# Down projection of whole batches by seven products of half width, in a linear attention and dense expert kernel

## The chip, the cores and the metric

The kernel runs on one core of a Trainium2 chip. The metric is device time in microseconds (us) of one execution; the time of a kernel is the median of its runs. One execution was also taken by the hardware profiler, and its trace gives the start and duration of every instruction on each engine: TensorE (PE, with its weight loads as PEld), VectorE (DVE), ScalarE (ACT), GpSimd (POOL) and SyncE (SP, which here only issues DMAs).

## The reference

Eight batches of 512 tokens of 128 channels go through a linear attention and then through eight dense experts; both are normalized and added to their input. Everything is fp32.

```python
def block(x):                                  # x: (8, 512, 128)
    x = x + layernorm(attn(layernorm(x)))
    return x + layernorm(ffn(layernorm(x)))

def attn(x):                                   # 4 heads of 32
    xn = layernorm(x) * gamma + beta
    q, k, v = split(xn @ w_qkv)
    k = softmax(k, over tokens)
    context = k^T v  (per head)
    return (q * 32**-0.5) @ context @ w_out + b_out + x

def ffn(x):                                    # 8 experts, 512 wide
    return sum(silu(x @ Wg[e]) * (x @ Wu[e]) @ Wd[e] for e in range(8))
```

## The kernel before

All expert weights stay in SBUF. The experts' work is cut into units: batches 0 and 7 are two units of 256 tokens each, batches 1 to 6 one unit of 512, ten units in all. A unit has 32 steps, one for each expert and each 128 of its 512 inner channels. A step (lines 621 to 639) makes g and u in PSUM on TensorE (lines 627 and 629, weights 128x128, the unit's tokens as columns), silu(g) on ScalarE (631), h = silu(g) * u on VectorE (633), and the down projection on TensorE (`down`, line 582), which adds wd^T h into one PSUM bank (acc) over all 32 steps. `down` is issued two steps late (LAG), so that h is ready. g and u have two PSUM banks each, acc one, everything else three (pool ps).

There is no scheduler: the order on each engine is the order in which the program issues, written by hand. `between(n)` is a set of generators; each step of the loop advances each of them by one `yield`, and so lays a piece of other work behind that step's h. While unit n runs its steps, `attention(b + 1)` prepares the next batch and `finish` ends the last one. `attention` normalizes x (statistics and application on VectorE, the reciprocal root as a power on GpSimd, lines 182 to 200), brings the tokens to channels, makes keys and their exponential (397 to 402), then g_ps, c_ps, m_ps, wa_ps (428 to 449), which fold context and output weights into one 128x128 matrix, and y (476); then follow two more normalizations with the residual on GpSimd (490) between them. `finish` normalizes the sum of the experts, adds the residual on GpSimd (529) and stores it.

Transpositions of batches 2 to 7 are made by VectorE in blocks of 32x32, and the blocks are brought to their places by `carry` (line 211): a store of the tile to DRAM and four loads from it, issued by SP. Generators wait LANDING steps for them. Batches 0 and 1 are transposed by TensorE. Batch 0's attention is a function of its own (`opening`) with nothing beside it. `finish_last` ends the last unit.

Of the kernel before, what the change touches and what calls it, by code (L numbers as in the profile page):

```python
# [1 line left out]

# [13 lines left out]
def kernel(  # L16
# [32 lines left out]

    nc = tc.nc  # L50
# [5 lines left out]
    Q = 32  # L56
    NQ = P // Q
    LANDING = 4
    BY_TENSORE = (0, 1)
# [8 lines left out]
    work = ctx.enter_context(tc.tile_pool(name="work", bufs=2))  # L68
    small = ctx.enter_context(tc.tile_pool(name="small", bufs=3))
    hp = ctx.enter_context(tc.tile_pool(name="hp", bufs=4))  # L70
    dram = ctx.enter_context(tc.tile_pool(name="dram", bufs=4, space=bass.MemoryType.DRAM))
# [3 lines left out]
    ps = ctx.enter_context(tc.tile_pool(name="ps", bufs=3, space=bass.MemoryType.PSUM))  # L75
# [74 lines left out]
    def keep_warm(moving, count=1):  # L150

        t = ps_acc.tile([P, N], F32, tag="acc", name="unread")
        for i in range(count):
            nc.tensor.matmul(
                t[:, : moving.shape[1]], moving[:, :P], moving,
                start=(i == 0), stop=(i == count - 1),
            )


    def norm_stats(src, name):  # L160

        n = src.shape[1]
        stats = small.tile([P, n, 6], F32, tag=f"stats{n}", name=f"stats_{name}")
        mv = small.tile([P, n, 2], F32, tag=f"mv{n}", name=f"mv_{name}")
        for j in range(n):
            nc.vector.bn_stats(stats[:, j, :], src[:, j])
# [8 lines left out]
    def pair_stats(src, name):  # L175
# [19 lines left out]
        return mv, rstd[:, :n], rstd[:, n:]  # L195

# [51 lines left out]
    def opening():  # L248
# [12 lines left out]
        v = const.tile([P, N], F32, name="v_0")  # L261
        qT = const.tile([P, N], F32, name="qT_0")
        x1 = work.tile([P, NJ, C], F32, tag="x1", name="x1_0")
        x1b = work.tile([P, NJ, C], F32, tag="x1b", name="x1b_0")
# [3 lines left out]
        yn = work.tile([P, NJ, C], F32, tag="yn", name="yn_0")  # L268
        z = work.tile([P, NJ, C], F32, tag="z", name="z_0")
        zT = work.tile([P, NQ, NJ, Q], F32, tag="zT", name="zT_0")  # L270
# [103 lines left out]
    def attention(b):  # L374
        xt = xs[b]
# [7 lines left out]
        if b in BY_TENSORE:  # L383
            xh_ps = transpose4(flat(xh), f"xh_ps_{b}")
            nc.scalar.activation(xnT, xh_ps, AF.Identity, bias=beta_sb, scale=gamma_sb)
        else:
            xhT = work.tile([P, NQ, P], F32, tag="xhT", name=f"xhT_{b}")
            to_channels(xh, xhT, f"xh_blk_{b}")
            for _ in range(LANDING):
                yield  # L390
            nc.scalar.activation(
                by_block(xnT), xhT.rearrange("c a (j i) -> c a j i", j=NJ),
                AF.Identity, bias=beta_sb, scale=gamma_sb,
            )
# [13 lines left out]
        x1b = work.tile([P, NJ, C], F32, tag="x1b", name=f"x1b_{b}")  # L408
# [4 lines left out]
        if b in BY_TENSORE:  # L413
            ek_ps = transpose4(ekT, f"ek_ps_{b}")
            nc.vector.tensor_copy(
                ek.rearrange("p b (j k) -> p j b k", j=NJ),
                ek_ps.rearrange("p (j b k) -> p j b k", j=NJ, b=NQ),
            )
            yield
            yield  # L420
        else:
            to_tokens(by_block(ekT), ek, f"ek_blk_{b}")
            for _ in range(LANDING):
                yield
# [26 lines left out]
        nc.vector.tensor_copy(wa, wa_ps[:, :C])  # L451
        yield
        x2 = xp.tile([P, NJ, C], F32, tag="x2", name=f"x2_{b}")
        x2s[b] = x2
        y = work.tile([P, NJ, C], F32, tag="y", name=f"y_{b}")
        yn = work.tile([P, NJ, C], F32, tag="yn", name=f"yn_{b}")
        z = work.tile([P, NJ, C], F32, tag="z", name=f"z_{b}")
        zT = work.tile([P, NQ, NJ, Q], F32, tag="zT", name=f"zT_{b}")
        lags = [after_wa(b, lo, hi, xt, xnT, wa, x1b, x2, y, yn, z, zT) for lo, hi in WHOLE]
        while lags:  # L460
            if next(lags[0], "end") == "end":
                lags.pop(0)
            for g in lags[1:]:
                next(g, None)
            yield

    def after_wa(b, lo, hi, xt, xnT, wa, x1b, x2, y, yn, z, zT):
        r = slice(lo, hi)
        y_ps = ps.tile([P, N], F32, tag="ps", name=f"y_ps_{b}_{lo}")
# [29 lines left out]
        if b in BY_TENSORE:  # L499
            yield  # L500
            z_ps = transpose4(flat(z[:, r]), f"z_ps_{b}_{lo}")
            for j in range(hi - lo if b == 0 and lo == 0 else 1):
                cp = nc.vector.tensor_copy if j else nc.scalar.copy
                if b or lo:
                    cp(zT[:, :, r], by_block(z_ps[:, : (hi - lo) * P], hi - lo))
                else:
                    cp(zT[:, :, j], z_ps[:, j * P : (j + 1) * P].rearrange("c (a i) -> c a i", a=NQ))  # L507
            zTs[b, lo] = zT[:, :, r]
        else:
            to_channels(z, zT.rearrange("c a j i -> c a (j i)"), f"z_blk_{b}")  # L510
            for lo, hi in parts(b):
                zTs[b, lo] = zT[:, :, lo:hi]

    def finish(b, lo, hi, f):
        r = slice(lo, hi)
        n = hi - lo
        if n < NJ:
            f_ps = transpose4(f, f"f_ps_{b}_{lo}")
            f3 = f_ps.rearrange("p (j b k) -> p j b k", j=NJ, b=NQ)[:, :n]
        else:  # L520
            for _ in range(LANDING if b + 2 < B else 2 * LANDING):
                yield
            f3 = f.rearrange("p b (j k) -> p j b k", j=NJ)
        s5 = norm_stats(f3, f"5_{b}_{lo}")
        yield
        fn = work.tile([P, NJ, C], F32, tag="fn", name=f"fn_{b}_{lo}")
        norm_apply(fn[:, :n].rearrange("p j (b k) -> p j b k", b=NQ), f3, s5)
        o = work.tile([P, NJ, C], F32, tag="o", name=f"o_{b}_{lo}")
        nc.gpsimd.tensor_tensor(flat(o[:, :n]), flat(fn[:, :n]), flat(x2s[b][:, r]), ALU.add)  # L529
        nc.sync.dma_start(out[b].rearrange("(p j) c -> p j c", j=NJ)[:, r], o[:, :n])  # L530

    def finish_last(b, lo, hi, acc):
# [9 lines left out]
        o = work.tile([P, NJ, C], F32, tag="o", name="o_last")  # L542
# [30 lines left out]
    accs, fTs, hs = {}, {}, {}  # L573
    pending = []

    def down(n, i):
        b, lo, hi = units[n]
        if i == 0:
            accs[n] = ps_acc.tile([P, N], F32, tag="acc", name=f"acc_{n}")
# [3 lines left out]
            accs[n][:, :cols], wd_sb[e][:, f, :], hs.pop((n, i)),  # L583
            start=(i == 0), stop=(i == NSTEP - 1),
        )
        if i == NSTEP - 1:
# [4 lines left out]
            acc = acc.rearrange("c (a j i) -> c a j i", a=NQ, j=hi - lo)  # L591
            if hi - lo < NJ:
                fT = work.tile([P, N], F32, tag="fT", name=f"fT_{n}")
                nc.vector.tensor_copy(by_block(fT[:, :cols], hi - lo), acc)
                fTs[n] = fT[:, :cols]
            else:
                fTs[n] = work.tile([P, NQ, P], F32, tag="f", name=f"f_{n}")
                to_tokens(acc, fTs[n], f"f_blk_{n}")

    def between(n):  # L600
# [8 lines left out]
        if hi == NJ and b + 1 < B:  # L609
            going.append(attention(b + 1))  # L610
        for i in range(NSTEP):
            if i == LAG + 1 and n > 0:
# [28 lines left out]
    while pending:  # L641
        down(*pending.pop(0))
# [31 lines left out]
```

## Time and profile before

| | |
|---|---|
| three runs | median 718.3 us, 718.03 to 719.45 |
| the profiled execution | 718.09 us, span of its instructions 716.0 us |
| granted TensorE clock, mean | 0.998 |
| opening, before the first g | 20.5 us |
| a whole batch, f transposition to f transposition (201.28 to 286.99) | 85.7 us |
| a step of a half batch (40.23 to 41.53) | 1.30 us |

In the profile a line such as `305.68 1.02 PE L627 MATMUL g<-zT,wg 128*128 128x512 f32 x2` is one group in order of time: start and duration in us, engine, line of the kernel, output and inputs, weights (rows*columns), output and how many records it has. A line of the list of groups ends with the busy time in us and the mean of one record in ns, and behind a second bar the time that the engine had been idle before these instructions, with what ended most of it. Groups with "+1 forms" mix 512 and 256 columns. The ends of matmuls are modelled, so that starts tell the pace.

### The profile page before, as it was taken

The numbers are of one execution on the slowest core, as the hardware profiler recorded it, in microseconds if no ns is written. First come the engines' busy times: TensorE is split into PE (matmuls) and PEld (weight loads), VectorE is DVE, ScalarE is ACT, GpSimd is POOL, SyncE is SP. The second block draws the span as 40 slices with busy tenths as digits, with TensorE's granted clock in tenths as the row PEclk, the third lists the DMA queues.
The fourth block names the chain that finished last, engine by engine and source line by source line (L and its number), as shares of the span: only waits on it lengthen the run. The fifth ranks groups of instructions, "written<-read, shape, count | busy, mean of one in ns | idle before, by whom it ended". The sixth has DMA issues, their size and how long they took to land. (4 is left out here: it accounts for less than half of the span.)

```text
span 716.0 us, 6760 instructions
## 1 busy us (share of the span) xinstructions
PE 706.1 (99%) x2189; PEld 398.4 (56%) x2189; DVE 312.3 (44%) x874; ACT 200.6 (28%) x377; POOL 75.1 (10%) x101
## 2 busy tenths in 40 slices
PE   8999999999999999999999999999999999999996
PEld 5788885444444544444444444444444454488885
DVE  5435545435245353444444444443534535243433
ACT  3323332422224222232223222242222422222221
POOL 3101111001002010010100110020100201000000
PEclk9999999999999999999999999999999999999999
DMA  8400000000111000110101101110001100000000
GB/s 267 148 1 0 23 1 24 28 16 0 45 59 45 1 22 22 60 45 0 45 15 44 45 0 45 39 36 30 0 29 45 44 15 12 18 31 15 8 1 8
DMA packets 27443, 23.83 MB, mean 33 GB/s; under 512 B 2960, under 2 KB 20624, under 8 KB 27408
## 3 DMA queue, kind: packets, MB, share of 16 engines
q1 hardware_dynamic: 27120, 23.21, 10.0%
q8 instruction: 17, 0.28, 0.2%
q10 hardware_dynamic: 288, 0.20, 0.1%
q14 instruction: 18, 0.15, 0.1%
HBM read 15.01 MB, written 8.39 MB: 33 GB/s over the span
## 5 line engine op out<-in xcount | busy, mean ns | idle before, releaser
L633 DVE TENSOR_TENSOR h<-sg,u 128x512 f32<-128x512 f32 (+1 forms) x320 | 185.1, 580 | 355.8 <-PE u L629 338.6
L631 ACT ACTIVATE sg<-g 128x512 f32<-128x512 f32 (+1 forms) x320 | 163.5, 511 | 481.1 <-PE g L627 442.6
L627 PE MATMUL g<-zT,wg 128*128 128x512 f32 (+1 forms) x640 | 272.6, 508 | 0.9 <-DVE zT L507 0.7
L629 PE MATMUL u<-zT,wu 128*128 128x512 f32 (+1 forms) x640 | 272.5, 507 | 0.2 <-DVE h L633 0.2
L582 PE MATMUL acc<-h,wd 128*128 128x512 f32 (+1 forms) x640 | 272.1, 507 | 0.1
L582 PEld LDWEIGHTS acc<-h,wd 128*128 128x128 f32 x640 | 121.5, 190 | 99.2 <-issue 91.8
L629 PEld LDWEIGHTS u<-zT,wu 128*128 128x128 f32 x640 | 121.3, 190 | 99.4 <-issue 86.0
L627 PEld LDWEIGHTS g<-zT,wg 128*128 128x128 f32 x640 | 118.4, 190 | 84.6 <-issue 77.0
L172 POOL TENSOR_TENSOR rstd<-ve,mhalf 128x4 f32<-128x4 f32 (+1 forms) x27 | 25.2, 933 | 356.4 <-DVE ve L170 356.3
L194 POOL TENSOR_TENSOR rstd<-ve,mhalf 128x8 f32<-128x8 f32 x7 | 11.5, 1636 | 184.3 <-DVE ve L187 184.3
L410 POOL TENSOR_TENSOR x1b<-x,bias_sb 128x128 f32<-128x128 f32 x28 | 12.1, 461 | 23.2 <-DVE x L200 23.2
L529 POOL TENSOR_TENSOR o<-fn,x 128x512 f32<-128x512 f32 (+1 forms) x9 | 9.8, 1084 | 19.8 <-DVE fn L200 18.9
L200 DVE TENSOR_SCALAR x<-x,mv,rstd 128x128 f32<-128x128 f32 x32 | 11.1, 406 | 0.1
L490 POOL TENSOR_TENSOR x<-yn,x 128x512 f32<-128x512 f32 (+1 forms) x8 | 9.6, 1199 | 12.2 <-DVE yn L200 10.8
L200 DVE TENSOR_SCALAR xh<-x,mv,rstd 128x128 f32<-128x128 f32 x32 | 8.8, 336 | 2.1 <-POOL rstd L194 1.8
L200 DVE TENSOR_SCALAR z<-x,mv,rstd 128x128 f32<-128x128 f32 x32 | 9.0, 341 | 1.3 <-POOL rstd L172 1.3
L168 DVE BATCH_NORM_AGGREGATE mv<-stats 128x2 f32<-128x6 f32 x94 | 9.3, 155 | 0.0
L402 ACT ACT_TABLE_LOAD x7 | 9.0, 1283 | 0.1
L631 ACT ACT_TABLE_LOAD x7 | 9.0, 1283 | 0.1
L428 PEld LDWEIGHTS g_ps<-ek,xh 128*128 128x128 f32 x56 | 7.4, 192 | 2.9 <-issue 2.9
L476 PEld LDWEIGHTS y_ps<-wa,xnT 128*128 128x128 f32 x56 | 7.4, 192 | 2.9 <-issue 2.9
L200 DVE TENSOR_SCALAR yn<-y,mv,rstd 128x128 f32<-128x128 f32 x28 | 7.8, 340 | 0.8 <-POOL rstd L172 0.8
(133 smaller groups left out, 202.4 us busy)
## 6 DMA issues: line engine op xcount, KB each, us to landing
wg<-in_L_ffn_Wg_dram SPq DMA_DIRECT2D x8, 256.0 KB, 6.0
wu<-in_L_ffn_Wu_dram SPq DMA_DIRECT2D x8, 256.0 KB, 5.9
wd<-in_L_ffn_Wd_dram SPq DMA_DIRECT2D x8, 256.0 KB, 6.1
x<-in_L_attn_x_dram SPq DMA_DIRECT2D x7, 256.0 KB, 2.8
bounce<-xh_blk SPq DMA_DIRECT2D x6, 256.0 KB, 2.0
xhT<-bounce SPq DMA_DIRECT2D x24, 64.0 KB, 2.0
bounce<-ek_blk SPq DMA_DIRECT2D x6, 256.0 KB, 2.0
ek<-bounce SPq DMA_DIRECT2D x24, 64.0 KB, 2.0
```

The costliest lines, as they stand in the source:

```text
L168: nc.vector.bn_aggr(mv[:, j, :], stats[:, j, :])
L172: nc.gpsimd.tensor_tensor(rstd, ve, mhalf[:, :n], ALU.pow)
L194: nc.gpsimd.tensor_tensor(rstd, ve, mhalf, ALU.pow)
L200: nc.vector.tensor_scalar(dst[:, j], src[:, j], mv[:, j, 0:1], rstd[:, j : j + 1], ALU.subtract, ALU.mult,)
L410: nc.gpsimd.tensor_tensor(x1b[:, j, :], x1[:, j, :], bias_sb, ALU.add)
L490: (nc.gpsimd if b or lo else nc.vector).tensor_tensor(flat(x2[:, r]), flat(yn[:, r]), flat(xt[:, r]), ALU.add)
L529: nc.gpsimd.tensor_tensor(flat(o[:, :n]), flat(fn[:, :n]), flat(x2s[b][:, r]), ALU.add)
L582: nc.tensor.matmul(accs[n][:, :cols], wd_sb[e][:, f, :], hs.pop((n, i)), start=(i == 0), stop=(i == NSTEP - 1),)
L627: nc.tensor.matmul(g_ps[:, :cols], wg_sb[e][:, w], zT, start=True, stop=True)
L629: nc.tensor.matmul(u_ps[:, :cols], wu_sb[e][:, w], zT, start=True, stop=True)
L631: nc.scalar.activation(sg[:, :cols], g_ps[:, :cols], AF.Silu)
L633: nc.vector.tensor_tensor(h[:, :cols], sg[:, :cols], u_ps[:, :cols], ALU.mult)
```

## The change

In whole batches the down projection no longer runs in every step. Two steps make a pair: their two blocks of 128 inner channels, the two halves of 64 output channels and the two halves of 256 tokens are the 2x2 blocks of a Strassen product (in Winograd's form). Seven products replace eight. Each has weights of 64 columns and moves 256 columns, and is put at the lower or upper 64 partitions of one of two PSUM banks (A and D), the two places in turn. Four of the products' weights are differences of wd blocks, made once by GpSimd in the first unit (`weight_sums`); four of the moving tiles are differences of h, made by GpSimd for each pair. Products of sixteen steps (eight pairs) are issued together, at step 17 of the unit and at step 1 of the next.

The results are put together only at the end: `Last.turn` transposes both banks (two carries instead of one), and `Last.add` adds the parts in seven VectorE operations.

Attention of batches 2 to 7 becomes a class whose pieces `plan(n)` puts at given steps, some of them a unit earlier (statistics, norm and transposition of x of batch b+2 in unit b). Their normalizations, and the last one of whole batches, are applied by ScalarE as x * rstd - mean * rstd, four instructions each, with the product mean * rstd on GpSimd. Batch 1 keeps the generator. Pools change: work tiles have one buffer instead of two, pool ps two PSUM buffers instead of three (the second half of batch 0's y takes one of u's), h and its differences nine pairs.

```diff
+    def norm_scalar(dst, src, rstd_nm, first=0):
+        rstd, nm = rstd_nm
+        for j, (d, t) in enumerate(zip(pieces(dst), pieces(src))):
+            i = first + j
+            nc.scalar.activation(
+                d, t, AF.Identity, bias=nm[:, i : i + 1], scale=rstd[:, i : i + 1]
+            )
...
+        def add(self):
+            A, D = (t.rearrange("p (t b) (s x) -> p t s b x", t=2, s=2) for t in self.f)
+            p1, p2, p4b, p6 = A[:, 0, 0], A[:, 0, 1], A[:, 1, 0], A[:, 1, 1]
+            p4, p7, p5 = D[:, 0, 0], D[:, 1, 0], D[:, 1, 1]
+            q = work.tile([P, 10, P // 2], F32, tag="q", name=f"q_{self.b}")
+            c11, c21, c12, c22, u = (q[:, 2 * i : 2 * i + 2] for i in range(5))
+            nc.vector.tensor_tensor(u, p1, p6, ALU.add)
+            nc.vector.tensor_tensor(c11, p1, p2, ALU.add)
+            nc.vector.tensor_tensor(p4, p4, p4b, ALU.add)
+            nc.vector.tensor_tensor(c21, u, p7, ALU.add)
+            nc.vector.tensor_tensor(c12, u, p5, ALU.add)
+            nc.vector.tensor_tensor(c22, c21, p5, ALU.add)
+            both = q[:, 2:6].rearrange("p (s b) x -> p s b x", s=2)
+            nc.vector.tensor_tensor(both, both, D[:, 0], ALU.add)
...
+    def weight_sums():
+
+        for e in range(E):
+            w = wd_sb[e].rearrange("p (q k) c -> p q k c", k=2)
+            a11, a21, a12, a22 = (w[:, :, k, c : c + HALF] for k in (0, 1) for c in (0, HALF))
+            t = ws_sb[e]
+            for i, (a, b, op) in enumerate((
+                (a21, a22, ALU.add), (t[:, :, 0], a11, ALU.subtract), (a11, a21, ALU.subtract),
+                (a12, t[:, :, 1], ALU.subtract),
+            )):
+                nc.gpsimd.tensor_tensor(t[:, :, i], a, b, op)
+                if i % 2:
+                    yield
...
+    def down_pairs(n, g, pairs):
+        b, lo, hi = units[n]
+        if g == 0:
+            accs[n] = [
+                ps_acc.tile([P, N], F32, tag=f"acc{t}", name=f"acc{t}_{n}") for t in "AB"
+            ]
+        A, D = accs[n]
+        low, high = slice(0, HALF), slice(HALF, C)
+        left, right = slice(0, N // 2), slice(N // 2, N)
+        last = NSTEP // 2 - 1
+        for two in range(0, len(pairs), 2):
+            below, above = [], []
+            for m, (h, t) in enumerate(pairs[two : two + 2]):
+                k = g * GROUP // 2 + two + m
+                e, pair = divmod(k, NF // 2)
+                w0, w1 = wd_sb[e][:, 2 * pair], wd_sb[e][:, 2 * pair + 1]
+                sm = ws_sb[e][:, pair]
+                first, end = k == 0, k == last
+                below += [
+                    (A[low, left], w0[:, low], h[:, 0], first, False),
+                    (A[low, right], w1[:, low], h[:, 2], False, end),
+                    (D[low, right], sm[:, 3], h[:, 3], first, end),
+                ]
+                above += [
+                    (D[high, right], sm[:, 0], t[:, 0], first, False),
+                    (A[high, right], sm[:, 1], t[:, 2], first, False),
+                    (D[high, left], sm[:, 2], t[:, 1], False, end),
+                ]
+                if m == 0:
+                    below.append((D[low, left], w1[:, high], t[:, 3], False, False))
+                else:
+                    above.append((A[high, left], w1[:, high], t[:, 3], False, end))
+            for two_tiles in zip(below, above):
+                for o, w, r, start, stop in two_tiles:
+                    nc.tensor.matmul(o, w, r, start=start, stop=stop)
+        if (g + 1) * GROUP == NSTEP:
+            fins[n] = Last(b, accs.pop(n))
...
+        following = attentions[b + 1] if 0 < b < B - 1 else None
+        second = opened(b + 2) if hi == NJ and b + 2 < B else None
+        last = None
+        if n and units[n - 1][2] - units[n - 1][1] == NJ:
+            last = lambda name: lambda: getattr(fins[n - 1], name)()
+            at(2, last("turn"))
+            at(3, last("turn"))
+        if following:
+            a = following
+            d = 4 if n == 2 else 0
+            at(1, a.keys)
+            for i in range(4, 8):
+                at(i + d, a.context)
+            at(8 + d, a.values)
+            at(9 + d, a.stats3)
+            at(10 + d, a.scales3)
+            at(12 + d, a.residual)
+            if d:
+                at(17, a.stats4, a.scales4)
+                at(19, a.norm4, a.turn4)
             else:
-                fTs[n] = work.tile([P, NQ, P], F32, tag="f", name=f"f_{n}")
-                to_tokens(acc, fTs[n], f"f_blk_{n}")
+                at(14, a.stats4)
+                at(15, a.scales4)
+        if hi < NJ or lo:
+            if second:
+                at(20, second.stats)
+                at(21, second.scales)
+                at(23, second.norm)
+                at(24, second.turn)
+                at(31, second.affine)
+            if last:
+                at(14, last("add"))
+                at(16, last("stats"))
+                at(18, last("scales"))
+                at(21, last("norm"))
+        else:
+            if second:
+                at(17, second.stats, second.scales)
+            if following and not d:
+                at(17, a.norm4, a.turn4)
+            if last:
+                at(17, last("add"), last("stats"), last("scales"))
+            if second:
+                at(17, second.norm, second.turn)
+                at(21, second.affine)
+            if last:
+                at(17, last("norm"))
+        return p
...
-            sg = hp.tile([P, N], F32, tag="sg", name=f"sg_{n}_{i}")
+            sg = sgp.tile([P, N], F32, tag="sg", name=f"sg_{n}_{i}")
             nc.scalar.activation(sg[:, :cols], g_ps[:, :cols], AF.Silu)
-            h = hp.tile([P, N], F32, tag="h", name=f"h_{n}_{i}")
-            nc.vector.tensor_tensor(h[:, :cols], sg[:, :cols], u_ps[:, :cols], ALU.mult)
-            hs[n, i] = h[:, :cols]
-            pending.append((n, i))
-            if len(pending) > LAG:
-                down(*pending.pop(0))
-            next(others, None)
+            if whole:
+                if i % 2 == 0:
+                    h2 = pairp.tile([P, 4, N // 2], F32, tag="h2", name=f"h2_{n}_{i}")
+                h = flat(h2[:, 2 * (i % 2) : 2 * (i % 2) + 2])
+            else:
+                h = hp.tile([P, N // 2], F32, tag="h", name=f"h_{n}_{i}")
+            nc.vector.tensor_tensor(h, sg[:, :cols], u_ps[:, :cols], ALU.mult)
+            if not whole:
+                due.append((count + LAG, partial(down, n, i, h)))
+            elif i % 2:
+                t2 = pairp.tile([P, 4, N // 2], F32, tag="t2", name=f"t2_{n}_{i}")
+                pairs.append((h2, t2))
+                if len(pairs) == GROUP // 2:
+                    due.append((count + LAG, partial(down_pairs, n, i // GROUP, pairs)))
+                    pairs = []
+            next(others)
+            while due and due[0][0] <= count:
+                due.pop(0)[1]()
+            if whole and i % 2:
+                nc.gpsimd.tensor_tensor(t2[:, 0:2], h2[:, 1::2], h2[:, 0:2], ALU.subtract)
+                nc.gpsimd.tensor_tensor(t2[:, 2], h2[:, 3], t2[:, 0], ALU.subtract)
+                nc.gpsimd.tensor_tensor(t2[:, 3], h2[:, 2], t2[:, 2], ALU.subtract)
+            count += 1
         for _ in others:
             pass
-    while pending:
-        down(*pending.pop(0))
+    for _, call in due:
+        call()
```

## The prediction

> **What bounds the kernel now.** I read the page's busy line and its row of slices first, then the costliest groups, then TensorE's order of time in three places: inside a whole batch, at the short matmuls of attention, and in a half batch.
>
> ```profile
> PE 706.1 (99%) x2189; PEld 398.4 (56%) x2189; DVE 312.3 (44%) x874; ACT 200.6 (28%) x377; POOL 75.1 (10%) x101
> ...
> PE   8999999999999999999999999999999999999996
> ```
>
> TensorE is busy from the second slice to the last but one, every other engine less than half of the span. A busy PE is not a PE at its peak, so the spacing of matmuls has to be seen:
>
> ```profile
> 299.67 1.02 PE L627 MATMUL g<-zT,wg 128*128 128x512 f32 x2
> 300.53 1.02 PE L629 MATMUL u<-zT,wu 128*128 128x512 f32 x2
> 301.38 1.02 PE L582 MATMUL acc<-h,wd 128*128 128x512 f32 x2
> 302.24 1.02 PE L627 MATMUL g<-zT,wg 128*128 128x512 f32 x2
> ...
> 321.13 1.05 PE L428 MATMUL g_ps<-ek,xh 128*128 128x128 f32 x8
> 322.02 1.02 PE L627 MATMUL g<-zT,wg 128*128 128x512 f32 x2
> ```
>
> ```profile
> 40.23 0.59 PE L627 MATMUL g<-zT,wg 128*128 128x256 f32 x2
> 40.66 0.59 PE L629 MATMUL u<-zT,wu 128*128 128x256 f32 x2
> ```
>
> ```profile
> 321.13 0.86 PEld L428 LDWEIGHTS g_ps<-ek,xh 128*128 128x128 f32 x7 [0.24 <-issue]
> ```
>
> Each fp32 matmul leaves two records (x2), each with its own weight load. From start to start a matmul takes 0.858 us with 512 columns (302.24 less 299.67, by 3), 0.4325 us with 256 (the half batches, 1.297 us per step of three) and 0.2225 us with 128 (0.89 by 4). That is proportional to the columns: TensorE streams without a gap. Seven weight loads of 128 columns in 0.86 us start (0.86 - 0.19) / 6 = 0.112 us apart, so loading keeps up even at 128 columns. The other engines' rows, for what follows:
>
> ```profile
> L633 DVE TENSOR_TENSOR h<-sg,u 128x512 f32<-128x512 f32 (+1 forms) x320 | 185.1, 580 | 355.8 <-PE u L629 338.6
> L631 ACT ACTIVATE sg<-g 128x512 f32<-128x512 f32 (+1 forms) x320 | 163.5, 511 | 481.1 <-PE g L627 442.6
> L582 PE MATMUL acc<-h,wd 128*128 128x512 f32 (+1 forms) x640 | 272.1, 507 | 0.1
> L490 POOL TENSOR_TENSOR x<-yn,x 128x512 f32<-128x512 f32 (+1 forms) x8 | 9.6, 1199 | 12.2 <-DVE yn L200 10.8
> L529 POOL TENSOR_TENSOR o<-fn,x 128x512 f32<-128x512 f32 (+1 forms) x9 | 9.8, 1084 | 19.8 <-DVE fn L200 18.9
> L410 POOL TENSOR_TENSOR x1b<-x,bias_sb 128x128 f32<-128x128 f32 x28 | 12.1, 461 | 23.2 <-DVE x L200 23.2
> ```
>
> VectorE and ScalarE wait for TensorE in the main loop, and TensorE waits for nobody. Only TensorE's own time counts.
>
> **The down projection.** In the six whole batches there are 32 steps each, 96 pairs of steps. A pair costs two down matmuls now, 2 x 0.858 = 1.716 us. It becomes seven products of 64 output rows and 256 columns, issued alternately to the array's lower and upper 64 columns. Call p the time of a couple, one product below and one above. A pair is 3.5 couples. No row of this trace has a matmul with 64 weight columns, so p is bounded from its neighbours:
> - Lower end 0.4325: both products run wholly beside each other, each streaming 256 columns as in the half batches. A smaller p is excluded, since each half of the array still streams its 256 columns at the pace of that row. Pair 1.514, 96 x (1.514 - 1.716) = -19.4 us.
> - Loading: a couple has four loads. If a load of 64 columns cost as much as one of 128, 4 x 0.112 = 0.448. Issuing: eight instructions a couple; the 128-column row shows four in 0.2225, so 0.445. Both lie just above the streaming time.
> - Upper end 0.865: one after the other. Pair 3.03, +126 us.
>
> A rule speaks against the change. The Trainium skill ("TensorE: Matmul & The Clock Gate", Part 3, measured speedup) has three column tiles at 512 columns gain 2.38 rather than 3, that is 0.79 of the ideal. By that p = 0.4325 / 0.79 = 0.545, a pair 1.91 us, and the products would cost +18.4 us. By the rows it is some -18. I side with the rows: 2.38 is given for a small pack of tiles, and in this trace a record lasts 0.592 us where the next starts after 0.429, so the tail that a lone pack pays is hidden in a stream; the blocks here are 28 couples long. I take p = 0.4375, between streaming (0.4325) and loading or issuing (0.445): pair 1.531, 96 x -0.185 = **-17.7 us**.
>
> **Switching.** The products come in twelve blocks (two per batch), so TensorE goes into column tiles and back 24 times. "TensorEngine Tiling (Array Packing)", Key Properties, says that changing the tiling mode drains TensorE; no run here shows it. Bounds: 0 each (it can't give time back), and the tail plus one exposed load, 0.163 + 0.190 = 0.353, together 8.5 us. The nearest row is a restart after a wait (at 20.47 us the first matmul took 0.54 to the next, 0.11 over its pace). I take 0.2: **+4.8 us**.
>
> **What it asks of GpSimd.** Each pair needs three subtractions there, one of 512 and two of 256 columns: by the rows of L490 (1.27 us at 512 when shapes are kept apart) and L529 (0.72 at 256) 2.71 us, and 96 x 2.71 = 260 us beside the 75 now. While g and u run alone a pair takes 4 x 0.858 = 3.43 us, so it fits with 0.7 us to spare; the reciprocal roots (1.0 to 1.6 us each) and residual additions borrow from it and the 12 us of a block pay back. The last pair's difference is ready about 0.9 + 2.7 us after its u; two more steps (3.4 us) are issued before the block and it comes last in the block, 9 us later still. h reads PSUM for u and should not be slowed by GpSimd. Cost 0; if GpSimd were 1.5 times as slow it would be 4.1 us per pair in a phase of 3.43, six pairs would fall 4 us behind, still inside the block's lead. The weight differences (32 of 128 columns, 0.46 us each, 15 us) lie in the first half batch, where GpSimd had 1.4 us to do in 39; the root for the second half's norm is queued behind four of them (1.8 us), which end at about 25.4 us, when its input comes at 25.7. Cost 0.
>
> **Norms on ScalarE, and the new places.** A normalization is four ACTIVATEs (0.39 us by the row of a 128x128 one) instead of four on VectorE (0.34), plus a small product on GpSimd. Without the down matmul a step lasts 1.716 us rather than 2.57; with two buffers, h may end some 2.57 us after its u and takes 0.9, so 1.7 us of VectorE work can stand between two h, and about as much before a Silu. The pieces put at single steps (0.7 to 1.6 us) fit. What doesn't is put at step 17, right ahead of the block: statistics, z's transposition, the seven additions that put the products together, their statistics, and three norms. Each waits for the other engine: VectorE is 9.0 us in it, ScalarE ends last at some 11.1 (its last norm waits for the root behind the additions). Silu of step 18 and h of step 18 are queued behind, and TensorE misses them only after the block (28 couples, 12.2 us) and two more steps (3.4 us): 15.6. At step 1 the keys (two table loads of 1.28, Exp 0.69, four norms) take 6 us under the other block. Cost 0; without that cover it would be up to 11 + 6 us a batch, 100 in all.
>
> SP issues one carry more per batch (five DMAs, about 4 us of latency by the present f carry's issues at 287.7 to 291.5); f isn't needed until step 14 or 17, z's carry starts at step 17 with 14 steps and more to go. Cost 0.
>
> Three places remain. u of step 1 waits for a PSUM bank that now holds the second half of batch 0's y until VectorE has normalized it, at 22.8 us by this trace where u began at 22.2: about +0.5. The first down matmul of batch 7 waits for the transposition of batch 6's sums out of the same bank: h (0.42), transposition (0.72), less two matmuls of 0.43: about +0.8. One PSUM buffer less for attention: its tiles follow each other step by step, 0. Together **+1.3 us**.
>
> **Sum.** -17.7 + 4.8 + 1.3 = -11.6 us. The profiled execution took 718.1 us (span 716.0 and 2.1 around it), 0.2 below the median of 718.3: 706.5 us, TensorE still the bound.
>
> **Rivals.**
> - *Slower: the halves run beside each other only in part.* Two records per product stand behind each other in one order. If the upper half's load is not taken until the lower half's second record has started, each change of side exposes a load: half of 0.112 if it goes by columns, twice per couple, p = 0.43 + 0.11 = 0.54 (the same as by the skill's 2.38): +16.7 + 4.8 + 1.3, 741 us; with whole loads 0.65 and 780. For it: no row of before shows a load taken past a waiting matmul, each starts with the matmul ahead of it. Against: loads overlap everywhere. It decides from p = (1.716 - 0.064) / 3.5 = 0.472, 35 ns over my value. 12 in 100.
> - *In between*, p 0.465 to 0.51 because issuing or loading is a little slower for small products: 713 to 730. 14 in 100.
> - *No overlap at all* (the change doesn't do what it says): 718 + 126 + 6 = 850. 4 in 100.
> - *The streams work, the cover doesn't*: step 17's chain outlasts 15.6 us, say by 2 us in each of six batches, or GpSimd holds up VectorE: 712 to 725. Busy shares speak against it. 4 in 100.
>
> **How the numbers follow.** The forecast holds 66 in 100, between 699 (p 0.4325, free switches) and 712 (p 0.448, 0.35 a switch). With the in-between and the cover cases 699 to 730 holds some 83. A measurement can tell 0.2% (1.4 us) from no change. Faster: 66, and 6 of the next ones, 72; same 3; slower 25.
>
> **What would show it.** Products as records of 128x64 weights, starting in twos, a couple each 0.43 to 0.45 us, blocks of 12 to 13 us; g and u at 0.858; gaps at a block's ends of 0.2; POOL busy near 350 us; no wait of g at step 20 for Silu. Wrong if a block takes over 13.7 us, if products alternate without overlapping, or if TensorE's idle time names ACT, DVE or POOL for more than a few us.

## The result and the profile after

The changed kernel takes **709.16 us** (median of four runs, 709.01 to 709.21) against 718.32 us for the kernel before on the same chip (718.03 to 719.45): ratio 0.987, 95% interval 0.985 to 0.989. The profiled execution took 709.01 us and its span is 707.1 us, 8.9 less than the 716.0 of before. The forecast was 706.5.

The busy line, the row of slices and one group of the page of the changed kernel:

```profile
PE 692.7 (98%) x3149; PEld 420.2 (59%) x3149; DVE 299.0 (42%) x832; ACT 247.8 (35%) x497; POOL 352.7 (50%) x445
...
PE   8998999999999999999999999999999999999996
...
L953 POOL TENSOR_TENSOR t<-h 128x512 f32<-128x512 f32 x96 | 121.9, 1270 | 117.6 <-DVE h L939 117.6
```

TensorE is still the bound. GpSimd went from 75 to 352.7 us; its first difference takes 1270 ns, as taken from before, and it waits for h, not h for it: the group of h has a mean of 581 ns, against 580 before. One slice in the row has dropped to 8, the fourth, 53 to 71 us; it comes back below.

A block of products inside a batch, TensorE in order of time (start, duration, line, output and inputs):

```profile
274.61 1.02 PE L534 MATMUL k_ps<-xnT,w_qkv_sb 128*128 128x512 f32 x2
275.56 0.43 PE L823 MATMUL accA<-h,wd 128*64 128x256 f32 x1
275.57 0.43 PE L823 MATMUL accB<-t,ws 128*64 128x256 f32 x1
...
276.04 0.38 PE L823 MATMUL accA<-h,wd 128*64 128x256 f32 x1
...
287.27 0.38 PE L823 MATMUL accB<-h,ws 128*64 128x256 f32 x1
...
287.80 1.12 PE L928 MATMUL g<-zT,wg 128*128 128x512 f32 x2
```

Records start in twos, at most 0.01 us apart, one in each half of the array. Between the second couple (276.04) and the 28th (287.27) lie 26 couples: 0.432 us each, the pace of one 256-column matmul alone (0.4325). Entry and exit cost time: k_ps should be followed at 274.61 + 0.858 = 275.47 and the first product starts at 275.56; the first couple takes 0.48, the last 0.53 to g, and g takes 0.96 to u instead of 0.858. That is 0.09 + 0.05 + 0.10 + 0.10 = 0.34 per block.

By this the streams give 96 x (3.5 x 0.432 - 1.7165) = -19.6 us and twelve blocks take back 12 x 0.34 = +4.1: -15.5. The span fell by 8.9 only. The rest is time that TensorE loses between its matmuls, idle or at a slower pace: summed from start to start over the whole program (gaps over 0.12 us beyond the pace, the block borders left out), the stretch behind the first g has 2.45 us of it before and 9.11 after, +6.7; the opening is 0.2 longer (first g at 20.68 against 20.47; in x3_split, with the same opening, it is at 20.42, so this is no effect of the change). -15.5 + 6.7 + 0.2 = -8.6.

The largest gap, TensorE in the second half of batch 0:

```profile
65.48 0.59 PE L930 MATMUL u<-zT,wu 128*128 128x256 f32 x2
68.74 0.69 PE L258 MATMUL f_ps<-ident,fT 128*128 128x128 f32 x2 [2.67 <-DVE fT L777]
69.22 1.06 PE L768 MATMUL acc<-h,wd 128*128 128x256 f32 x2
70.08 1.06 PE L928 MATMUL g<-zT,wg 128*128 128x256 f32 x2
```

f_ps, a transposition, waits for fT, the copy of the first unit's sums that VectorE makes. u to f_ps takes 3.26 us instead of 0.43: a gap of 2.83. Behind it the matmuls come at 0.86 instead of 0.43 us. The reason is the clock, in a table of stretches (PE, PEld, DVE, ACT, POOL busy with records, then the granted clock, the DMA share and GB/s):

```profile
64.85:68.26 3.41, 1.22 (x6) 0.74 (x4) 1.91 (x11) 0.38 (x1) 1.65 (x1) 1.00 0.00 0
68.26:71.68 3.42, 2.94 (x8) 2.41 (x9) 1.63 (x8) 0.38 (x1) 0.70 (x1) 0.50 0.00 0
```

For 3.42 us TensorE was granted half its clock. VectorE's order in both kernels shows why f_ps came late. After:

```profile
67.24 1.11 DVE L249 TENSOR_SCALAR xh<-x,mv,rstd 128x128 f32<-128x128 f32 x4 [1.43 <-POOL rstd L208]
68.26 0.42 DVE L777 COPY fT<-acc 128x256 f32<-128x256 f32 x1
```

Before:

```profile
65.52 0.42 DVE L594 COPY fT<-acc 128x256 f32<-128x256 f32 x1
...
67.01 1.12 DVE L200 TENSOR_SCALAR xh<-x,mv,rstd 128x128 f32<-128x128 f32 x4 [1.08 <-POOL rstd L194]
```

The two have changed places. xh, batch 1's norm, waits for GpSimd's root in both. Now the copy stands behind it on VectorE, f_ps stands behind the copy on TensorE, and acc, g and u behind f_ps. The smaller gaps that are new stand behind the u of 97.01 (z_ps, 0.72 against 0.18), behind the u of 121.08 and of 123.80 (f_ps and g of the first whole unit, 0.73 and 0.34), and ahead of the first down matmul of batch 7 (1.47), shown here with VectorE's instruction before it:

```profile
619.28 0.71 DVE L602 STREAM_TRANSPOSE f_blkA<-accA 128x512 f32<-128x512 f32 x1
...
620.14 0.67 PE L768 MATMUL acc<-h,wd 128*128 128x256 f32 x2 [1.30 <-DVE f_blkA L602]
```

### The profile page after: what moved, and what is told of

The parts are those of the page before. It is cut to its first block, busy times and chain, and to the rows that moved or that the text cites. A ratio compares the mean times of both kernels' runs of the same rounds, so it can differ in the third digit from the quotient of the medians.

```text
span 707.1 us, 9148 instructions
## 1 busy us (share of the span) xinstructions
PE 692.7 (98%) x3149; PEld 420.2 (59%) x3149; DVE 299.0 (42%) x832; ACT 247.8 (35%) x497; POOL 352.7 (50%) x445
## 4 chain that ended last, share of the span: by engine, by line
PE 93%; DVE 2%; issue 2%; POOL 1%; ACT 1%; DMA 0%; DVEq 0%; POOLq 0%
PE g L928 31%; PE u L930 30%; PE accA L823 12%; PE accB L823 9%; PE acc L768 7%; PE y_ps L559 1%; PE g_ps L476 1%; PE k_ps L534 1%; POOL rstd L186 0%; DMA x<-in_L_attn_x_dram 0%; DVE stats L180 0%; PE z_ps L258 0%; POOL x L450 0%; DVE stats L196 0%; POOL rstd L208 0%
## 5 line engine op out<-in xcount | busy, mean ns | idle before, releaser
L953 POOL TENSOR_TENSOR t<-h 128x512 f32<-128x512 f32 x96 | 121.9, 1270 | 117.6 <-DVE h L939 117.6
L823 PE MATMUL accB<-t,ws 128*64 128x256 f32 x384 | 107.0, 381 | 0.0
L823 PE MATMUL accA<-h,wd 128*64 128x256 f32 x384 | 99.2, 381 | 0.0
L768 PE MATMUL acc<-h,wd 128*128 128x256 f32 x256 | 76.4, 381 | 1.3 <-DVE f_blkA L602 1.3
L954 POOL TENSOR_TENSOR t<-h,t 128x256 f32<-128x256 f32 x96 | 69.7, 726 | 7.5
L955 POOL TENSOR_TENSOR t<-h,t 128x256 f32<-128x256 f32 x96 | 69.6, 725 | 7.5
L823 PEld LDWEIGHTS accA<-h,wd 128*64 128x64 f32 x384 | 51.6, 137 | 34.7 <-issue 4.9
L823 PE MATMUL accA<-t,ws 128*64 128x256 f32 x192 | 57.1, 379 | 0.0
L823 PE MATMUL accB<-h,ws 128*64 128x256 f32 x192 | 57.1, 379 | 0.0
L768 PEld LDWEIGHTS acc<-h,wd 128*128 128x128 f32 x256 | 47.9, 191 | 9.0 <-issue 3.1
L823 PEld LDWEIGHTS accB<-t,ws 128*64 128x64 f32 x384 | 51.6, 137 | 0.0
```

The costliest lines, as they stand in the source:

```text
L768: nc.tensor.matmul(accs[n][:, :cols], wd_sb[e][:, f, :], h, start=(i == 0), stop=(i == NSTEP - 1))
L823: nc.tensor.matmul(o, w, r, start=start, stop=stop)
L953: nc.gpsimd.tensor_tensor(t2[:, 0:2], h2[:, 1::2], h2[:, 0:2], ALU.subtract)
L954: nc.gpsimd.tensor_tensor(t2[:, 2], h2[:, 3], t2[:, 0], ALU.subtract)
L955: nc.gpsimd.tensor_tensor(t2[:, 3], h2[:, 2], t2[:, 2], ALU.subtract)
```

## The experiments

Two theories of the missing time (15.5 us gained by the products, 8.9 seen) were tried against each other first: that it lies in the order of the half batches' queues (mine), or in the products themselves (switching, or pairs that GpSimd holds up). Then came the sizes of the prediction's own terms. All diffs are against the changed kernel; all ratios are to the kernel before.

**e1_order.** In half batches the loop advances the other work before it issues the due down matmul; here the down matmul goes first.

```diff
+            while due and due[0][0] <= count and due[0][1].func is down:
+                due.pop(0)[1]()
             next(others)
```

> Edit: in half batches the down matmul that is due is issued ahead of the step's other pieces, as before the change, so that the copy fT of the finished sums stands on VectorE ahead of batch 1's xh and, one unit on, ahead of the keys' transposition. My theory (the missing 6 us are VectorE's queue order around the half batches): the wait of f_ps at 65.5 us (2.83 us, and 1.3 us of slow matmuls behind it), the 1.2 us at 121 to 125 and 0.4 at 97 go, 704.2 us, between 703.6 and 704.8. Rival (f_ps is simply issued two steps too early, whatever VectorE's order): no gain over 1 us, 708.2 to 709.2. Rival (the new load of GpSimd and ScalarE slows the half batches): no change, 709.2.

Measured 708.18 us (707.99 to 708.29), ratio 0.986 (0.985 to 0.988). A miss of 4 us. The last down of a unit is now issued before the pieces of the same step, so the generator that ends that unit starts one step earlier still, and TensorE comes to f_ps before its copy is done at all three places where f of a half batch is transposed beside other work:

```profile
66.05 0.44 PE L258 MATMUL f_ps<-ident,fT 128*128 128x128 f32 x2 [0.99 <-DVE fT L777]
```

The gap here, from acc at 64.47, is 1.15; others are 0.92 at 115.65 and 0.68 at 658.70, and g behind the u of 120.71 waits 1.77 for Silu. The one wait was broken into several. The clock stayed whole (mean 0.998 against 0.995), and that is nearly all that was gained: the gaps sum to 8.3 us, while of the changed kernel's 9.1 some 1.4 are slow matmuls and 7.7 waits.

**e2_finish.** The end of the unit before starts at step 3 instead of step 2.

```diff
-            if isinstance(fins.get(n - 1), type(weight_sums())):
+            if i > LAG and isinstance(fins.get(n - 1), type(weight_sums())):
```

> Edit: only the finish of a half batch starts at step 3 instead of 2, so that f_ps comes a step later; the copy fT stays behind xh on VectorE. My theory: the first down matmul of the new unit needs the bank that fT reads, so the wait moves from f_ps to it and hardly shrinks: 708.6 to 709.3 us. Rival (f_ps too early is the cause): 4 us less, 705.

Measured 708.29 us, ratio 0.987 (0.985 to 0.988); the four runs are two pairs, 707.27 and 707.44 at a mean clock of 0.997 to 0.998, 709.14 and 709.20 at 0.996. The wait didn't go: it moved from f_ps to the first down matmul of the new unit, which writes the bank that fT is copied from, and is 2.83 us again (at 65.38). In the profiled run (707.44) no halved clock follows it; so, by the mean clocks, the 1.8 us between the pairs are the halved clock, and the slower pair takes as long as the changed kernel.

**e3_order_finish.** Both edits.

> Edit: both of the two edits above. My theory: 703.9 us, a few tenths under the order alone (f_ps no longer waits the last 0.2 us). Rival of the early f_ps: 705. Rival of engine load: 709.2.

Measured 705.41 us (705.25 to 706.60), ratio 0.983 (0.981 to 0.984), 3.8 us below the changed kernel; neither edit alone had given more than 1. The waits of f_ps are gone, and those at the acc beside it (0.29) and at z_ps (0.18) are what they were before the change. What is left over is one wait of the first whole unit and batch 7's 1.46:

```profile
119.67 0.38 PE L258 MATMUL f_ps<-ident,fT 128*128 128x128 f32 x2
121.44 1.12 PE L928 MATMUL g<-zT,wg 128*128 128x512 f32 x2 [1.39 <-ACT sg L932]
```

It is the wait for Silu of unit 2 behind batch 2's keys at step 1. In later batches a block lies over that step; unit 2 follows a half batch and has none. So this was 1.5 us above what I had expected.

**e4_warm.** The waits stay, but six matmuls that nothing reads are put ahead of f_ps, so that TensorE works while it would wait.

```diff
+        if b == 0 and lo == 0:
+            unread = ps_acc.tile([P, N], F32, tag="accB", name="unread_f")
+            for k in range(6):
+                nc.tensor.matmul(
+                    unread[:, : N // 2], warm[:, :P], warm, start=(k == 0), stop=(k == 5)
+                )
```

> Edit: the changed kernel with six unneeded matmuls (256 columns, 2.6 us) issued into an idle PSUM bank in front of f_ps, where TensorE waits 2.8 us; everything else as it is. The trace shows matmuls at half their pace for 3 us behind that wait. Theory that the idle stretch itself halves the granted clock: matmuls behind it keep their pace, about 1.2 us less, 708.0 us, although work is added. Rival (they are slow because of what VectorE still does, or the gap is too short to matter): 709.2, or up to 0.3 more.

Measured 707.25 us (707.24 to 707.35), ratio 0.985 (0.983 to 0.986): 1.9 us less, by adding work.

```profile
68.54 0.44 PE L258 MATMUL f_ps<-ident,fT 128*128 128x128 f32 x2
68.81 0.60 PE L774 MATMUL acc<-h,wd 128*128 128x256 f32 x2
69.25 0.59 PE L934 MATMUL g<-zT,wg 128*128 128x256 f32 x2
```

f_ps starts as late as it did, 3.26 us after u's start then (65.48 to 68.74) and now (65.28 to 68.54), but acc to g takes 0.44 instead of 0.86. So the halved clock by itself cost 1.5 (half of the 2.94 us that were busy in it) to 1.9 us, and the wait 2.83.

**e5_best.** Both orders, and the two other waits: the first bank of batch 6 is transposed right at the end of its last block, and batch 2's norm of x1 is moved from step 1 to step 7.

```diff
         if (g + 1) * GROUP == NSTEP:
             fins[n] = Last(b, accs.pop(n))
+            if units[n + 1][2] - units[n + 1][1] < NJ:
+                fins[n].turn()
...
-            at(2, last("turn"))
+            if hi - lo == NJ:
+                at(2, last("turn"))
...
             d = 4 if n == 2 else 0
             at(1, a.keys)
+            if d:
+                at(7, a.first_norm)
```

> Edit: the version with both order edits, and two more. The last batch's half: bank A of batch 6's sums is transposed right behind its last block and not after h of step 2, so that the first down matmul of batch 7 waits for it less (1.46 us now). Unit 2, the only one whose keys have no block over them: the four ScalarE instructions that make x1 move from step 1 to step 7 (g waits 1.4 us for Silu there now). Theory that these queue orders are all that is left: 705.4 less 1.3 and 1.0, 703.1 us. Rival (the waits only move on): 705.

Measured **702.20 us** (702.18 to 703.54), ratio 0.978 (0.977 to 0.979): the fastest of all, 6.96 below the changed kernel. Its gaps behind the first g sum to 2.48 us, against 2.45 in the kernel before. Three places in its profile:

```profile
120.87 0.38 PE L258 MATMUL f_ps<-ident,fT 128*128 128x128 f32 x2
121.11 1.13 PE L938 MATMUL g<-zT,wg 128*128 128x512 f32 x2
...
614.36 0.59 PE L940 MATMUL u<-zT,wu 128*128 128x256 f32 x2
614.79 0.64 PE L773 MATMUL acc<-h,wd 128*128 128x256 f32 x2
```

f_ps to g takes 0.24, and u to batch 7's first down 0.43, where it had been 1.77 in e3_order_finish and 1.90 in the changed kernel. The products were left as they were, so the missing time lay in the order of queues around them. (The profiled execution is the one of 703.54 us; its first g starts at 21.85, 1.2 later than in the changed kernel.)

**x1_serial.** In each two pairs the seven lower products come first, then the seven upper ones.

```diff
-            for two_tiles in zip(below, above):
-                for o, w, r, start, stop in two_tiles:
-                    nc.tensor.matmul(o, w, r, start=start, stop=stop)
+            for o, w, r, start, stop in below + above:
+                nc.tensor.matmul(o, w, r, start=start, stop=stop)
```

> Edit: the same products in another order: in each two pairs first the seven of the lower 64 columns, then the seven of the upper ones, instead of one below and one above in turn. Theory that the gain needs two products beside each other, and that matmuls start in order: a block takes 56 x 0.4325 = 24.2 us less some overlap at eight changes of side (up to 1.7), instead of 12.2; twelve blocks, +125 to +145 us, 834 to 854 us. Rival (TensorE finds the partner itself, or the gain is only fewer columns): 709.

Measured 785.44 us (two runs, 784.81 and 786.07), ratio 1.094 (1.091 to 1.096): +76.3, 6.4 per block, against +125 or more that I expected of wholly serial products. Two pairs take 4.44 us (344.12 to 348.56), between 3.02 (seven couples) and 6.05 (fourteen products in a row). At each change of side four of fourteen records overlap:

```profile
344.12 0.81 PE L822 MATMUL accA<-h,wd 128*64 128x256 f32 x3
344.56 0.43 PE L822 MATMUL accB<-t,ws 128*64 128x256 f32 x1
344.77 0.38 PE L822 MATMUL accA<-h,wd 128*64 128x256 f32 x1
...
344.99 0.38 PE L822 MATMUL accB<-h,ws 128*64 128x256 f32 x1
...
345.48 1.03 PE L822 MATMUL accB<-t,ws 128*64 128x256 f32 x4
```

The upper half's first record (344.56, from t and a ws difference) starts ahead of lower ones that the program issues before it (344.77, 344.99). The same happens at the change back (346.78). So a record of the other half starts up to three records before its turn, and no further in this order: seven products in a row are too many. Whether an order coarser than couples but within that reach would lose nothing was not tried.

**x2_plain.** The blocks keep their places and GpSimd its work, but they hold plain matmuls of 128 weight columns and 512 moved ones; the differences go unread, so the output is not the reference's.

```diff
...
+            for s in range(2):
+                nc.tensor.matmul(
+                    accs[n][k % 2], wd_sb[e][:, 2 * pair + s], flat(h[:, 2 * s : 2 * s + 2]),
+                    start=(k < 2 and s == 0), stop=(k >= last - 1 and s == 1),
+                )
```

> Edit: the blocks, their places and all other work stay, but a block holds the plain down matmuls (128x128 weights, 512 columns, two per pair, alternating between the banks) in place of the seven products. The output is not the reference's: the parts are still put together as if they were the seven products, and GpSimd's differences go unread. Theory that the gain is the products' streaming alone: 96 x (1.7165 - 3.5 x 0.431) = 20.0 us more, no changes of tiling 4.1 less: 725.1 us. Rival (part of the gain comes from leaving down out of the steps, or the new order of attention): under 722. Rival (the order costs on its own): the same 725, and above the 718.3 of before by 6.8, which the sum of the waits seen (6.4 more than before) also gives.

Measured 724.49 us (723.07 to 724.60), ratio 1.009 (1.007 to 1.010). The products are worth 724.49 - 709.16 = 15.3 us with their switching, where the starts gave 15.5; everything else in the change costs 724.49 - 718.32 = 6.2, where the gaps and the opening gave 6.9.

**x3_split.** Each block is issued as two halves with one step's g and u between them: 24 changes of tiling more. (Batch 6's first transposition comes early here too, the others a step later.)

```diff
...
-                    due.append((count + LAG, partial(down_pairs, n, i // GROUP, pairs)))
+                    due.append((count + LAG, partial(down_pairs, n, i // GROUP, pairs[:4])))
+                    due.append((count + LAG + 1, partial(down_pairs, n, i // GROUP, pairs[4:], 4)))
```

> Edit: each block of eight pairs is issued as two of four, with g and u of one step between them; the same products, 24 more changes between column tiles and the whole array (and bank A of the last whole batch transposed a little earlier, worth up to 1.3 us). The trace of the changed kernel shows about 0.17 us lost at each change. Theory that a change costs this wherever it stands: +4.1, less 1.3: 712.0 us, 711.5 to 713.3. Rival (blocks may be as short as one likes): 708 to 709.2. Rival (a change costs the whole tail and load, 0.35): 716.

Measured 711.06 us (710.80 to 712.42), ratio 0.990 (0.989 to 0.992): +1.9. That is a little less than expected, and two savings are in it. Its profile has no halved clock behind the same 2.84 us wait (1.5 to 1.9 saved, as in e4_warm). And batch 7's first down still waits for the transposition, since the second half of the block now ends right ahead of it, but 0.9 us instead of 1.47:

```profile
620.77 0.38 PE L823 MATMUL accB<-h,ws 128*64 128x256 f32 x1
...
621.23 0.72 DVE L602 STREAM_TRANSPOSE f_blkA<-accA 128x512 f32<-128x512 f32 x1 [5.74 <-PE accA L823]
...
622.00 0.70 PE L768 MATMUL acc<-h,wd 128*128 128x256 f32 x2 [0.85 <-DVE f_blkA L602]
```

So 24 changes cost 1.9 + (1.5 to 1.9) + 0.6 = 4.0 to 4.4 us, 0.17 to 0.18 each. Between the halves, g (323.84) to u (324.80) takes 0.96 and u to the first product (325.75) 0.95 instead of 0.858 each, the same signs as at a whole block's ends. By starts a change costs 0.17 (0.34 per block), which agrees.

**x4_pool.** GpSimd makes the first difference of each pair twice: 96 x 1.27 = 122 us of work more.

```diff
                 nc.gpsimd.tensor_tensor(t2[:, 0:2], h2[:, 1::2], h2[:, 0:2], ALU.subtract)
+                nc.gpsimd.tensor_tensor(t2[:, 0:2], h2[:, 1::2], h2[:, 0:2], ALU.subtract)
```

> Edit: GpSimd makes the first difference of each pair (512 columns, 1.27 us) twice, 3.98 us a pair instead of 2.71, where a pair of g, u steps takes 3.43. Theory that GpSimd's work is covered by the blocks' lead: 709.2 to 711 us; the 122 us more of GpSimd work don't show, except where the roots behind it delay step 17's chain past the block. Rival (GpSimd already bounds a phase, or holds up VectorE): +1.2 us per pair in a phase, 12 phases of 7 pairs, up to 100 us, at least 8 us.

Measured 714.05 us (712.74 to 714.45), ratio 0.994 (0.992 to 0.995): +4.9, between the two expectations. A pair takes GpSimd 4.19 us (215.52 to 219.71) while g and u bring one every 3.43, and the blocks don't wait for it; what its backlog delays is the small products that the norms need (here nm of y):

```profile
229.47 1.65 ACT L242 ACTIVATE y<-y,nm,rstd 128x128 f32<-128x128 f32 x4 [1.47 <-POOL nm L235]
```

Silu of the next step stands behind y, and TensorE loses about 0.5 us a batch (at 314.45 and 319.00 in one) and 0.9 in unit 2. In the changed kernel itself GpSimd has most of that room: 122 us more cost 4.9.

**x5_late.** The pieces of step 17 go to step 20, behind the block instead of under it.

```diff
-                at(17, second.stats, second.scales)
+                at(20, second.stats, second.scales)
...
-                at(17, a.norm4, a.turn4)
+                at(20, a.norm4, a.turn4)
...
-                at(17, last("add"), last("stats"), last("scales"))
+                at(20, last("add"), last("stats"), last("scales"))
...
-                at(17, second.norm, second.turn)
-                at(21, second.affine)
+                at(20, second.norm, second.turn)
+                at(25, second.affine)
...
-                at(17, last("norm"))
+                at(20, last("norm"))
```

> Edit: in whole batches the pieces of step 17 that stand ahead of a block are put at step 20, behind it (and the xnT of step 21 at 25); nothing else. In the changed kernel ScalarE ends this chain 9.6 us after u of step 17, under a block of 12.2. Theory that the block is their cover: Silu of step 21 ends 10.2 us after u of step 20, and TensorE runs out of work after 3.4: 6.8 us a batch in five batches, one or two in the first, and perhaps a halved clock behind each wait (1.9 us): 744 to 755 us. Rival (the waits for the other engines are short anyway, the place does not matter): 709 to 715.

Measured 759.5 us (755.84 to 760.83), ratio 1.056 (1.053 to 1.059): +50.3.

```profile
268.84 2.08 PE L928 MATMUL g<-zT,wg 128*128 128x512 f32 x2 [6.20 <-ACT sg L932]
270.71 1.91 PE L930 MATMUL u<-zT,wu 128*128 128x512 f32 x2
```

u stands at 261.62. The gaps for Silu are 6.36 in four batches (one of them is shown), 3.30 in the first and 5.39 in the last, 34.1 together. Each is followed by matmuls at half the clock (g to u 1.87 here instead of 0.858; mean clock of the run 0.969), which is the remaining 16 us, some 2.7 a batch. The cover is real, and the waits are as long as expected (6.8 a batch in five batches and one or two in the first); the total missed the expected 744 to 755 by 4.5 us, since half the clock cost 2.7 behind each wait and not 1.9.

## Why the prediction was right, and where it was not

The time lies in the range and on the side given, 2.7 us above the forecast, which is the balance of two terms that were too dear (by 1.9 and 0.7 us) and one far too cheap (by 5.6, the opening with it). The mechanism, couples at the pace of one matmul, was right; that the total came so near is in part luck, since the errors offset each other by half.

- **The couple.** The value taken was 0.4375; it is 0.432, the lower end. The streams gave 19.6 instead of 17.7. Issuing and loading, which I had put at 0.445 to 0.448, don't show: the 64-column loads lie wholly beside the products. The rule that spoke against the change (2.38 for three column tiles, the Trainium skill, "TensorE: Matmul & The Clock Gate", Part 3) would have given 0.545; two tiles in a stream of 28 couples gain 2.00 here, so its 0.79 doesn't carry over to this stream. The rows were the better guide.
- **Switching.** Taken 0.2 a change, measured 0.17 by starts (4.1 us instead of 4.8) and 0.17 to 0.18 by the time of 24 more. The nearest row, a restart with 0.11 over its pace, was near in size. That each change costs something agrees with what the Trainium skill says of a drain ("TensorEngine Tiling (Array Packing)", Key Properties); that these 0.17 us are a drain, no run here shows.
- **GpSimd.** 352.7 us busy where 75 + 260 + 15 had been summed, no wait of TensorE for its new work (the root that xh waits for at 67.24 was nearly as late before, 67.01). Its limit, once it exceeds the phase's 3.43 us, lies in the norms' small products and not in the blocks (x4_pool), which the prediction's "still inside the block's lead" didn't see.
- **The cover of step 17.** The first and the last of ScalarE's three norms there:

```profile
317.66 1.63 ACT L242 ACTIVATE z<-x,nm,rstd 128x128 f32<-128x128 f32 x4
...
325.82 1.65 ACT L242 ACTIVATE fn<-q,nm,rstd 128x128 f32<-128x128 f32 x4 [1.50 <-POOL nm L235]
```

  It ends at 327.47, 9.6 us after u is through (316.97 + 0.86 = 317.83) (11.1 had been said), under a block of 12.2. No g waits at step 20. x5_late shows what the cover is worth: 50 us with the clock that goes with it.
- **Two sums.** The range's ends, 699 and 712, leave out the +1.3 of the three places, and p of 0.465 makes 715.7 us and not 713. Neither bears on the result.
- **The step that was mis-sized: "Three places remain … Together +1.3 us".** Measured +6.7 of gaps, most of it idle time that names VectorE, which the prediction itself had put among the signs of its being wrong. u of step 1 cost nothing (0.22 at mb_ps in both kernels) instead of 0.5, and batch 7's first down 1.47 instead of 0.8: from u's start it is 0.70 to h, 0.34 on to the transposition and 0.86 on to the down matmul, 1.90 less u's own 0.43, where I had taken only the two durations and had two matmuls to set against them. Missing from the list were f_ps of the first half batch (2.83 and the halved clock behind it, against 0.29 before: +3.8), z_ps (+0.5), and unit 2's keys and f_ps (+1.1), where "At step 1 the keys … take 6 us under the other block" holds for every whole unit but the first. I followed the order of queues through the whole batches, where the change was made, and not through the half batches, whose loop it rewrote as well. e3_order_finish and e5_best show that this is the cause: with the order mended and the two other places covered, the gaps are back at 2.48 and the time is 702.2, near -15.5 from 718.3.

What stays open: of the single sources of +6.7 only the sum was removed (e5_best); z_ps's 0.54 was not tried by itself. Why the halved clock follows the 2.8 us wait in some runs and not in others, the traces tell in the main (last section), but not where exactly the limit lies.

## What to carry to other kernels

Two matmuls of half the weight columns, issued in turn to the two halves of the array, cost the time of one in a long stream (28 couples here); count their streaming time, and about 0.17 us each time the tiling changes. When a change rewrites the loop, follow the order of every engine's queue through the units that it does not mean to touch, above all the first one of a new kind: here the kernel gave back 6.7 of 15.5 us there. A wait of 2.8 us on TensorE can be worth up to 4.7, since the clock may be halved behind it; whether it is can differ from run to run of one kernel, so compare the granted clock before a difference of 1 to 2 us is put down to an edit.

## What the runs showed of the hardware that was not expected

- TensorE doesn't start matmuls strictly in program order when they go to different column halves: in x1_serial a record of the upper half starts at 344.56, ahead of lower records of 344.77, 344.99 and 345.20 that are issued before it, three in advance. The Trainium skill ("TensorE: Matmul & The Clock Gate", Part 3, the mechanism) has matmuls monotone in start and end; the starts of this trace disagree (ends are modelled and can't tell).
- 2.67 us without a running matmul were enough for 3.42 us at half the clock, where the same page (Part 1, what is happening) speaks of an idle window of about 3.4 us. In e1_order a wait of 0.99 was not followed by it; in e2_finish 2.67 was, by the mean clock, in two of four runs.
- Why in some and not in others: in these traces the granted clock changes only on a fixed beat. In the changed kernel it changes at 68.26, 71.68 and 703.14 us, in x5_late at 69.72, 73.13, 175.53, 182.36, 267.69 and so on, always whole multiples of 3.413 us apart; the beat lies elsewhere in each run. What the runs differ in is how long TensorE was idle within one such stretch. The stretch that holds most of the same wait, in x4_pool and then in e2_finish, each with the next one (columns as in the table above):

```profile
66.49:69.90 3.41, 1.32 (x7) 1.22 (x8) 2.58 (x11) 0.00 (x0) 0.55 (x1) 1.00 0.00 0
69.90:73.31 3.41, 3.41 (x11) 2.78 (x11) 1.13 (x4) 1.28 (x3) 1.42 (x2) 0.50 0.00 0
```

```profile
64.23:67.65 3.42, 1.75 (x9) 1.19 (x7) 1.93 (x12) 0.77 (x2) 1.65 (x1) 1.00 0.00 0
67.65:71.06 3.41, 2.42 (x14) 2.19 (x15) 1.85 (x7) 0.76 (x2) 0.00 (x0) 1.00 0.00 0
```

  TensorE was idle for 3.41 - 1.32 = 2.09 us of the stretch in x4_pool, 2.19 in the changed kernel and 2.48 in x5_late, and the next stretch ran at half the clock (the figure before the last two of a row). In e2_finish the wait falls on two stretches, 1.67 and 0.99, and the clock stayed. So it did with 1.60 in x3_split and 1.88 in x2_plain. One stretch doesn't fit a limit near 2 us: at the end of the changed kernel (699.73 to 703.14), with two transpositions in it, 1.63 us were idle and the clock fell. So idle time is not the whole rule.
- A wait of 6.2 us (x5_late, from 262.64) was followed by two such stretches at half the clock, 267.69 to 274.52, the first beginning 1.15 us before the wait ends.
